# A graph attention layer over 196 groups of edges: gathering every group, shorter look-ahead, and maxima in three parts

## The chip, the cores and the metric

The kernel runs on one core of a Trainium2 chip. The metric is the device time of one execution in microseconds (us). The core's engines are named as in the profile: PE (TensorE, matrix products; PEld are its weight loads), DVE (VectorE), ACT (ScalarE), POOL (GpSimd, which here issues the indirect loads) and SP (SyncE, which issues most other loads and stores). Each works through its own list of instructions in order, and waits where one needs something that another engine or a transfer has not yet delivered.

## The reference

3125 nodes with 128 features, 100000 edges sorted by destination, 5 relations, 8 heads of 16. For each relation, a softmax over the edges that arrive at a node weighs the sources' values; the sums go through a projection, a residual and two normalisations. Cut to what matters:

```python
x_src = node_embeddings[src]
x_dst = node_embeddings[dst]
for r in range(R):
    mask = edge_types == r
    q = jnp.einsum('eh,khd->ekd', x_dst, W_Q[r])
    k = jnp.einsum('eh,khd->ekd', x_src, W_K[r])
    v = jnp.einsum('eh,khd->ekd', x_src, W_V[r])
    logits = (q * k).sum(-1) / scale + attn_bias[r][None, :]
    masked_logits = jnp.where(mask[:, None], logits, NEG)
    max_v = jax.ops.segment_max(masked_logits, dst, num_segments=n)
    exp_l = jnp.where(mask[:, None], jnp.exp(masked_logits - max_v[dst]), 0.0)
    sum_exp = jax.ops.segment_sum(exp_l, dst, num_segments=n)
    attn = exp_l / (sum_exp[dst] + 1e-12)
    out = out + jax.ops.segment_sum(attn[:, :, None] * v, dst, num_segments=n)
```

## The kernel before

**Tables first.** For every node and relation, k and v (256 numbers, 1 KB) and q (in three bf16 parts) are computed once and stored in DRAM (`kv_d`, `q_d`). The preparation, up to about 111 us, makes the table of k and v for all 25 blocks of 128 nodes (`table`, L398), the first three blocks of q, and the lists of indices and of destinations.

**Groups and steps.** The edges are cut into 196 groups of 512, each held as 128 partitions by T = 4 columns. The main loop (L1124) counts steps k. In step k the group g = k gets its logits, and an older group v gets its softmax weights and sums:

- `gather(g)` (L694): four indirect loads on POOL, one a column, each bringing 128 rows of k and v from `kv_d` into a buffer `kvs_[g % KVB]`. There are KVB = 23 buffers. Before the loop the first KVA = 9 groups are gathered (L1121); then in step k the loop gathers up to the group of step k + AHEAD, AHEAD = 3 (L1150), in the last steps one step ahead.
- `fetch_keys`, `fetch_q` (SP): the group's keys and a window of 128 rows of `q_d`, three steps ahead. `spot` (DVE, L795) makes one-hot matrices `hot`, `spread_q` (PE, L804, 12 matmuls) spreads q over the edges, `logits` (DVE, L817 and L818) multiplies by k and sums over each head, `store_logits` (SP, L823) writes them to `lg_d`.
- When all edges of a block of 128 nodes have logits (step `full_step[b]`, called F below, every 8 steps), `maxima_load(b)` in step F + 1 fetches for each node its run of up to 64 edges' logits (`ell`, one indirect load on POOL, L830). On POOL it stands behind the gathers of its step. `maxima(b, c0, c1)` computes the relations' maxima: ACT copies `ell` into `by_head` (PSUM, L845), DVE makes a mask `mine` (L853), for each relation a row `shut` (L863), adds (`wl`, L868) and reduces (`mx`, L874); the last part also rounds into three bf16 pieces (L879 to L889). It is called with relations 0 to 2 in step F + 3 and 3 to 4 in step F + 4 (`ready[b]` is F + 8). `store_m` writes the result in step F + 5.
- 16 to 19 steps after its logits, a group is weighed: `spread_m` (PE, L921) spreads the maxima, `less_max` (DVE, L930), `exps` (ACT, L934), `weigh` (DVE, L939, the last reader of the group's buffer), `sums` (PE, L973) with a carry between groups, `norm` (DVE, L994 to L997), `by_node` (ACT, L1007). The first weighing is in step 16.

Within a step DVE's order is: weigh, less_max, norm, logits, spot, pieces of q's later blocks, then maxima, then normalisations of finished blocks.

**The XG groups.** Groups 3, 6, 9, 12 and 15 (`XG`, L62) are not gathered from the table. Their source nodes' x is gathered during the preparation (L653 to L658) into buffers that exist from the start, together with those of groups 0, 1, 2 and 4. Five steps before such a group is due, PE turns x (`turn_x`, L764), DVE makes five copies masked by relation (`by_relation`, L771, `xm`), PE multiplies them with the weights (`products`, L782, `pk`) and ACT copies k and v into the buffer (`put_kv`, L791), spread over four steps, with the edges' types loaded by SP (L757).

Of the kernel before, what the change touches and what calls it, by code (L numbers as in the profile page):

```python
# [17 lines left out]
P = 128  # L18
N = 3125
NT = 25  # L20
NP = NT * P
R = 5
HEADS = 8
HD = 16
H = 128
# [5 lines left out]
KVW = 2 * H  # L31
# [8 lines left out]
GE = 512  # L40
T = GE // P
NGR = -(-E // GE)
# [6 lines left out]
RH = 3  # L49
# [1 line left out]
LW = HEADS + 1  # L51
PW = H + HEADS
FAR = 4000
AHEAD = 3
LAG = 8
LAG_H = 7
HALVED = 0
# [1 line left out]
NSR = E // SR  # L59
SB = P * E // N // SR  # L60
SPAD = 5
XG = range(3, 16, 3)  # L62
QB = 3
KVB = 23
HELD = 21
KVA = 9

# [66 lines left out]
def windowed_path(  # L134
# [4 lines left out]
    nc = tc.nc  # L139
# [11 lines left out]
    def keep(name, shape, dt=F32):  # L151
        return const.tile(shape, dt, name=name)
# [15 lines left out]
    lift = keep("lift", [1, H])  # L168
    wq = keep("wq", [P, R, H])
    wkv = keep("wkv", [P, R, 2, H])  # L170
    xi = keep("xi", [P, len(XG), T], I32)

    kvs_ = {}

    def buffers(those):
        for i in those:
# [1 line left out]
                [P, T, KVW], F32, name=f"kv{i}"  # L178
            )


    at_once = [*(g for g in range(5) if g not in XG), *XG]
    buffers(at_once)
    ahead = ctx.enter_context(tc.tile_pool(name="ahead", bufs=3))

# [7 lines left out]
    xn = load.tile([P, NT, H], F32, name="xn")  # L193
    nc.vector.memset(xn[:, NT - 1, :], 0.0)
    nc.sync.dma_start(xn[:, :4, :], x[: 4 * P].rearrange("(i p) h -> p i h", p=P))
    nc.sync.dma_start(
        xi,
        src[: (NGR - 1) * GE].rearrange("(g p t) -> p g t", p=P, t=T)[
            :, XG.start : XG.stop : XG.step, :
        ],  # L200
    )
    fr = load.tile([1, NGR + NSR], I32, name="fr")
    with nc.allow_non_contiguous_dma(reason="one element of each group"):
        nc.sync.dma_start(
# [30 lines left out]
    ident = keep("ident", [P, P])  # L235
# [125 lines left out]
    live = {}  # L361
# [287 lines left out]
        15: [sorted_rows],  # L649
        17: [sorted_ends],  # L650
    }

    for i, g in enumerate(XG):  # L653
        for t in range(T):
            nc.gpsimd.indirect_dma_start(
                out=kvs_[g][:, t, H:], out_offset=None, in_=x[:, :],
                in_offset=bass.IndirectOffsetOnAxis(ap=xi[:, i, t : t + 1], axis=0),
            )  # L658
    rows, counted = {}, 0
    xT = {b: turn(b) for b in range(2)}  # L660
    for b in range(NT):
# [27 lines left out]
    ps = ctx.enter_context(tc.tile_pool(name="ps", bufs=2, space=PSUM))  # L689
# [2 lines left out]
    flow = ctx.enter_context(tc.tile_pool(name="flow", bufs=2))  # L692
    late_flow = ctx.enter_context(tc.tile_pool(name="late_flow", bufs=2))
    def gather(g):  # L694
        if g in XG:
            return
        kv = kvs_[g % KVB]
        for t in range(T):
            nc.gpsimd.indirect_dma_start(  # L699
                out=kv[:, t, :], out_offset=None, in_=kv_d[:, :],  # L700
                in_offset=bass.IndirectOffsetOnAxis(ap=idx[:, t, g : g + 1], axis=0),
            )
# [43 lines left out]
    def store_q(b):  # L746
# [8 lines left out]
    def fetch_types(g):  # L755
        tr = ahead.tile([P, GE], I32, name="tr", bufs=1)
        nc.sync.dma_start(tr, edge_type[g * GE : (g + 1) * GE].partition_broadcast(P))  # L757
        live["tr", g] = tr

    def turn_x(g):  # L760
        xe = kvs_[g % KVB][:, :, H:]
        tx = ps.tile([P, T, P], F32, name="tx", tag="me")
        for t in range(T):
            nc.tensor.transpose(tx[:, t, :], xe[:, t, :], ident)  # L764
        live["tx", g] = tx

    def by_relation(g):
        tr, tx = live.pop(("tr", g)), live.pop(("tx", g))
        xm = late_flow.tile([P, R, T, P], F32, name="xm", tag="wl", bufs=1)
        for r in range(R):  # L770
            nc.vector.scalar_tensor_tensor(  # L771
                xm[:, r], tr.rearrange("h (p t) -> h t p", t=T), float(r), tx,
                op0=ALU.is_equal, op1=ALU.mult,
            )
        live["xm", g] = xm

    def products(g, t0):
        xm = live["xm", g]
        pk = ps.tile([P, 2, KVW], F32, name="pk", tag="me")
        for t in range(2):  # L780
            for r in range(R):
                nc.tensor.matmul(  # L782
                    pk[:, t, :], xm[:, r, t0 + t, :], wkv[:, r].rearrange("h s c -> h (s c)"),
                    start=(r == 0), stop=(r == R - 1),
                )
        if t0:
            live.pop(("xm", g))
        live["pk", g, t0] = pk

    def put_kv(g, t0):  # L790
        nc.scalar.copy(kvs_[g % KVB][:, t0 : t0 + 2, :], live.pop(("pk", g, t0)))  # L791

    def spot(g):
        hot = hold.tile([WR, T, P], BF16, name="hot")
# [281 lines left out]
    step_of, n = {}, 0  # L1076
# [24 lines left out]
    root_at = {b: d + 2 for b, d in done_at.items()}  # L1101
# [4 lines left out]
    norm_at = {b: r + (r < final - 1) for b, r in root_at.items()}  # L1106


    x_at = {g: step_of[g] - 5 for g in XG}
    assert min(x_at.values()) >= -2 and max(x_at.values()) + 2 < at_k[0] - 1  # L1110
# [10 lines left out]
    for gathered in range(KVA):  # L1121
        gather(gathered)
    assert all(q_from[b] >= 2 for b in range(QB, NT))
    for k in range(-4, root_at[NT] + 2):  # L1124
        v, g = v_at.get(k), group_at.get(k)
        q_step = {k - f: b for b, f in enumerate(q_from) if b >= QB and -2 <= k - f <= 5}

        if k >= 0 and k + 3 in group_at:
            fetch_keys(group_at[k + 3])
            fetch_q(group_at[k + 3])  # L1130
        if -2 in q_step:
            fetch_x("xq", q_step[-2])
        for b in range(NT):
            if done_at[b] - 1 == k:
                fetch_x("xr", b)
            if norm_at[b + 1] + 1 == k:
                store_z(b)
        for b in range(NM):
            if ready[b] - 3 == k:
                store_m(b)  # L1140
        if 5 in q_step:
            store_q(q_step[5])
        for u in range(NGR):
            if max(at_k[u] - 3, ready[block_of(u, MEND)] - 2) == k:
                fetch_m(u)
        for u in XG:
            if x_at[u] - 2 == k:
                fetch_types(u)

        while gathered < NGR - 1 and step_of[gathered + 1] <= k + (AHEAD if k < final - 16 else 1):  # L1150
            gathered += 1
            gather(gathered)
        for b in range(NM):
            if full_step[b] + 1 == k:
                maxima_load(b)

        for u in XG:
            if x_at[u] + 2 == k:
                put_kv(u, 0)
                put_kv(u, 2)  # L1160
        for b in range(NT):
            if done_at[b] + 1 == k:
                residual(b)
        if v_at.get(k - 4) is not None:
            by_node(v_at[k - 4])
        if v_at.get(k - 2) is not None:
            carry(v_at[k - 2])
        if 1 in q_step:
            turned(q_step[1])
        if 3 in q_step or 4 in q_step:  # L1170
            second_part()
        if 2 in q_step or 3 in q_step:
            first_part()

        if v_at.get(k + 1) is not None:
            spread_m(v_at[k + 1], 8 if k + 1 in group_at else 12)
        if v_at.get(k - 1) is not None or v_at.get(k - 3) is not None:
            sums(v_at.get(k - 1), v_at.get(k - 3))
        if k + 1 in group_at:
            spread_q(group_at[k + 1])  # L1180

        if v is not None:
            weigh(v)
        if v_at.get(k + 1) is not None:
            less_max(v_at[k + 1])
            exps(v_at[k + 1])
        if v is not None:
            weights(v)
        if k + 1 in group_at:
            types(group_at[k + 1])  # L1190
        if v_at.get(k - 2) is not None:
            norm(v_at[k - 2])
        if g is not None:
            logits(g)
            store_logits(g)
        if k + 2 in group_at:
            spot(group_at[k + 2])
        if v_at.get(k + 1) is not None:
            places(v_at[k + 1], 2 if k >= final - 1 else 0)
        if 3 in q_step or 4 in q_step:  # L1200
            third_part()
        if 2 in q_step or 3 in q_step:
            remainder()
        for b in range(NM):
            whole = MB[b][2] is None
            if ready[b] - 5 == k and whole:
                maxima(b, 0, RH)
            if ready[b] - 4 == k:
                maxima(b, RH if whole else 0, R)
        for b in range(NT):  # L1210
            if done_at[b] == k:
                project(b)
        for b in range(NT + 1):
            if root_at[b] == k:
                roots(b)
            if norm_at[b] == k:
                norms(b)
        for u in XG:
# [517 lines left out]
```

## Time and profile before

| | us |
|---|---|
| median of 3 runs | 1664.48 |
| lowest, highest | 1659.51, 1679.92 |
| the profiled execution, its own time | 1665.2 |
| its span in the profile | 1663.5 |

| engine | busy us | share of the span | instructions |
|---|---|---|---|
| PE | 1043.0 | 63% | 7746 |
| PEld | 790.5 | 48% | 7746 |
| DVE | 945.4 | 57% | 2536 |
| ACT | 638.7 | 38% | 2258 |
| POOL | 796.5 | 48% | 901 |

No engine is busy all the time. In the profile's other parts, a line such as `L699 POOL DMA_INDIRECT kv<-kv_d,idx x764 | 724.5, 948 | 587.9` names a line of the kernel, the engine, the operation, what it writes and reads, how often; then the busy time in us, the mean of one in ns, and how long the engine was idle just before. For an indirect load POOL's time is that of issuing it, not of the transfer. The mean granted clock of PE was 0.724 of full speed.

The groups that the change touches:

| group | count | busy us | mean ns |
|---|---|---|---|
| L699 kv gathers, POOL | 764 | 724.5 | 948 |
| L655 x gathers for XG, POOL | 20 | | 944 (median) |
| L830 ell, POOL | 25 | 23.6 | 944 |
| L782 pk, PE | 200 | 62.9 | 448 |
| L868 wl, DVE | 49 | 73.1 | 1491 |

### The profile page before, as it was taken

How to read it: one execution, taken by the hardware profiler on the slowest of the kernel's cores; microseconds unless marked ns; L12 is line 12 of the kernel's file. 1: busy time of each engine (PE TensorE's matmuls, PEld its weight loads, DVE VectorE, ACT ScalarE, POOL GpSimd, SP SyncE). 2: the span in 40 equal slices, each digit the busy share in tenths (PEclk: the TensorE clock that was granted, in tenths of full speed). 3: DMA queues.
4: the chain of work that ended last, by engine and by line, in shares of the span. 5: the costliest groups of instructions: out<-in, count | busy, mean ns of one | idle time of the engine just before them, and what ended most of it. 6: DMA issues, size and time to landing. Idle time of an engine off the chain costs nothing.

```text
span 1663.5 us, 26129 instructions
## 1 busy us (share of the span) xinstructions
PE 1043.0 (63%) x7746; PEld 790.5 (48%) x7746; DVE 945.4 (57%) x2536; ACT 638.7 (38%) x2258; POOL 796.5 (48%) x901
## 2 busy tenths in 40 slices
PE   6774836356566666665666666666566655665676
PEld 2443624245454444554554554555445544454564
DVE  3452626455564665556466555657555564564686
ACT  1450103144344444434445443444344343334344
POOL 6345061645465545545645554555455455445400
PEclk8885967677676767667676766777666776666878
DMA  6683343445455544544545454555445444444400
GB/s 161 232 309 105 72 134 80 108 124 137 101 135 126 132 110 121 137 109 118 144 118 129 126 137 107 137 131 131 108 120 139 109 122 120 107 118 108 102 16 15
DMA packets 181946, 203.66 MB, mean 122 GB/s; under 512 B 83943, under 2 KB 146819, under 8 KB 181676
## 3 DMA queue, kind: packets, MB, share of 16 engines
q0 software_dynamic: 40576, 112.08, 23.4%
q1 hardware_dynamic: 136790, 85.12, 21.9%
q10 hardware_dynamic: 4430, 4.71, 1.1%
q8 instruction: 64, 1.05, 0.3%
q14 instruction: 86, 0.70, 0.1%
HBM read 166.51 MB, written 35.28 MB: 121 GB/s over the span
## 4 chain that ended last, share of the span: by engine, by line
PE 29%; DVE 28%; issue 19%; another core or an unknown queue 10%; ACT 5%; DMA 2%; SPq 1%; DVEq 0%; ACTq 0%; POOL 0%
PE pp L973 9%; PE qe L804 4%; PE me L921 4%; DVE wl L868 4%; DVE mx L874 4%; DVE prod L817 4%; PE pk L782 3%; DVE wv L939 3%; DVE lg L818 2%; PE pp L975 2%; PE pr L404 2%; ACT at L959 2%; DVE hot L795 2%; PE prq L725 1%
## 5 line engine op out<-in xcount | busy, mean ns | idle before, releaser
L699 POOL DMA_INDIRECT kv<-kv_d,idx x764 | 724.5, 948 | 587.9 <-DVE den L994 346.6
L973 PE MATMUL pp<-wv,at 128*125 128x136 f32 x1568 | 392.7, 385 | 43.3 <-issue 34.1
L973 PEld LDWEIGHTS pp<-wv,at 128*125 128x125 f32 x1568 | 295.7, 256 | 122.4 <-issue 116.0
L804 PE MATMUL qe<-qw,hot 125*128 125x128 bf16 x2352 | 229.9, 256 | 87.7 <-issue 77.6
L921 PE MATMUL me<-mw,hot 125*128 125x64 bf16 (+1 forms) x2352 | 145.3, 217 | 217.6 <-issue 115.2
L804 PEld LDWEIGHTS <-hot 125*128 125x128 bf16 x2352 | 203.3, 125 | 99.6 <-issue 86.3
L921 PEld LDWEIGHTS <-hot 125*128 125x128 bf16 x2352 | 126.6, 113 | 253.5 <-issue 197.0
L934 ACT ACTIVATE me<-me 128x32 f32<-128x32 f32 x196 | 35.7, 182 | 542.0 <-DVE me L930 409.5
L959 ACT ACTIVATE at<-row_at,nkey 128x125 f32<-128x125 f32 x744 | 237.6, 398 | 0.0
L930 DVE TENSOR_TENSOR me<-lg,me 128x32 f32<-128x32 f32 x196 | 37.7, 193 | 348.6 <-remote 195.6
L939 DVE TENSOR_TENSOR wv<-kv,me 128x512 f32<-128x512 f32 x196 | 133.0, 679 | 104.0 <-remote 63.2
L817 DVE TENSOR_TENSOR prod<-kv,qe 128x512 f32<-128x512 f32 x196 | 132.9, 678 | 43.2 <-PE qe L804 25.7
L818 DVE TENSOR_REDUCE lg<-prod 128x32 f32<-128x512 f32 x196 | 134.5, 686 | 6.8
L975 PE MATMUL pp<-pt,carried 125*5 125x136 f32 x390 | 101.4, 350 | 57.8 <-ACT pt L988 27.4
L962 ACT ACTIVATE at<-at 128x500 f32<-128x500 f32 (+1 forms) x196 | 117.3, 599 | 6.2
L725 PE MATMUL prq<-wq,xTq 128*128 128x384 f32 (+1 forms) x88 | 52.7, 693 | 92.9 <-DVE hot L795 61.1
L1007 ACT COPY oT<-pp 128x25 f32 x196 | 33.7, 172 | 180.6 <-PE me L921 72.8
L830 POOL DMA_INDIRECT ell<-lg_d,start_i x25 | 23.6, 944 | 154.3 <-DMA lg_d<-lg 62.0
L782 PE MATMUL pk<-wkv,xm 128*128 128x256 f32 x200 | 62.9, 448 | 50.3 <-issue 46.3
L868 DVE TENSOR_TENSOR wl<-by_head,shut 128x1536 f32<-128x1536 f32 (+2 forms) x49 | 73.1, 1491 | 33.7 <-PE pk L782 25.6
L982 PEld LDWEIGHTS pp<-rsum,o 125*128 125x128 f32 x392 | 83.6, 257 | 14.0 <-issue 13.3
L982 PE MATMUL pp<-rsum,o 125*128 125x25 f32 x392 | 74.2, 270 | 12.8 <-issue 8.2
(191 smaller groups left out, 1199.5 us busy)
## 6 DMA issues: line engine op xcount, KB each, us to landing
kt<-key_d SPq DMA_DIRECT2D x196, 128.0 KB
qw<-q_d SPq DMA_DIRECT2D x196, 96.0 KB
kv_d<-kvs SPq DMA_DIRECT2D x24, 640.0 KB
kv<-kv_d,idx POOLq DMA_INDIRECT x764
q_d<-q SPq DMA_DIRECT2D x22, 480.0 KB
lg_d<-lg SPq DMA_DIRECT2D x196, 18.0 KB
mw<-m_d SPq DMA_DIRECT2D x196, 6.0 KB
xr<-in_x SPq DMA_DIRECT2D x24, 64.0 KB
```

What stands on the lines that cost most here:

```text
L699: nc.gpsimd.indirect_dma_start(out=kv[:, t, :], out_offset=None, in_=kv_d[:, :], in_offset=bass.IndirectOffsetOnAxis(ap=idx[:, t, g : g + ...
L804: nc.tensor.matmul(qe[:, t, :], hot[:, t, :], qw[:WR, s, :], start=(s == 0), stop=(s == 2))
L817: nc.vector.tensor_tensor(prod, kv[:, :, :H], live.pop(("qe", g)), op=ALU.mult)
L818: nc.vector.tensor_reduce(lg[:, :, :HEADS], prod.rearrange("p t (k d) -> p t k d", d=HD), AX.X, ALU.add)
L868: nc.vector.tensor_tensor(wl, by_head[:, None].to_broadcast([P, n, nh, D]), shut[:, :n, None, :].to_broadcast([P, n, nh, D]), op=ALU.add,)
L921: nc.tensor.matmul(me[:, t], hot[:, t, :], mw[:WR, None, :, s, :].to_broadcast([WR, times, 2, HEADS // 2]), start=(s == 0), stop=(s == 2),)
L939: nc.vector.tensor_tensor(wv[:, :, :H].rearrange("p t (k d) -> p t k d", d=HD), kv[:, :, H:].rearrange("p t (k d) -> p t k d", d=HD), live ...
L959: nc.scalar.activation(at[:, t, :], row_at[:, :WR], AF.Abs, bias=nkey[:, t, g : g + 1], scale=1.0)
L962: nc.scalar.activation(at[:, on_dve:], at[:, on_dve:], AF.Relu, bias=1.0, scale=-1.0)
L973: nc.tensor.matmul(pp, at[:, t, :], wv[:, t, :], start=(t == 0), stop=(t == T - 1))
L975: nc.tensor.matmul(pp[:R], carried[:WR, g, :], live.pop(("pt", g - 1)), start=False, stop=False,)
L982: nc.tensor.matmul(op, live.pop(("o5", done)), rsum[:WR], start=True, stop=True)
```

## The change

1. `XG` and all that belongs to it is taken out: the list of indices `xi` and its load, the 20 gathers of x, `fetch_types`, `turn_x`, `by_relation`, `products`, `put_kv` and their places in the loop. Groups 3, 6, 9, 12 and 15 are gathered from `kv_d` like the others. The buffers that exist from the start are now those of groups 0 to 8, and all nine of these groups are gathered before the loop.
2. `AHEAD` goes from 3 to 2, `KVB` from 23 to 22.
3. The maxima of a whole block are computed in three parts: relations 0 and 1 in step F + 2, 2 and 3 in step F + 3, 4 and the rounding in step F + 4.

```diff
-AHEAD = 3
+AHEAD = 2
...
-XG = range(3, 16, 3)
 QB = 3
-KVB = 23
+KVB = 22
...
-    at_once = [*(g for g in range(5) if g not in XG), *XG]
+    at_once = range(KVA)
...
-    nc.sync.dma_start(
-        xi,
-        src[: (NGR - 1) * GE].rearrange("(g p t) -> p g t", p=P, t=T)[
-            :, XG.start : XG.stop : XG.step, :
-        ],
-    )
...
-    for i, g in enumerate(XG):
-        for t in range(T):
-            nc.gpsimd.indirect_dma_start(
-                out=kvs_[g][:, t, H:], out_offset=None, in_=x[:, :],
-                in_offset=bass.IndirectOffsetOnAxis(ap=xi[:, i, t : t + 1], axis=0),
-            )
...
     def gather(g):
-        if g in XG:
-            return
         kv = kvs_[g % KVB]
...
-    x_at = {g: step_of[g] - 5 for g in XG}
...
-    for k in range(-4, root_at[NT] + 2):
+    for k in range(-2, root_at[NT] + 2):
...
-        for u in XG:
-            if x_at[u] + 2 == k:
-                put_kv(u, 0)
-                put_kv(u, 2)
...
+            if ready[b] - 6 == k and whole:
+                maxima(b, 0, 2)
             if ready[b] - 5 == k and whole:
-                maxima(b, 0, RH)
+                maxima(b, 2, 4)
             if ready[b] - 4 == k:
-                maxima(b, RH if whole else 0, R)
+                maxima(b, 4 if whole else 0, R)
...
-        for u in XG:
-            if x_at[u] == k:
-                turn_x(u)
-                by_relation(u)
-            if x_at[u] + 1 == k:
-                products(u, 0)
-                products(u, 2)
```

More of the change, by code (lines that the diff above doesn't have):

```diff
@@ L170, in windowed_path @@
     wkv = keep("wkv", [P, R, 2, H])
-    xi = keep("xi", [P, len(XG), T], I32)
     kvs_ = {}
@@ L751, in store_q @@
         )
[L755 to L791, printed above, removed]
     def spot(g):
@@ L1106, in windowed_path @@
     norm_at = {b: r + (r < final - 1) for b, r in root_at.items()}
-    x_at = {g: step_of[g] - 5 for g in XG}
-    assert min(x_at.values()) >= -2 and max(x_at.values()) + 2 < at_k[0] - 1
     q_from = []
@@ L1145, in windowed_path @@
                 fetch_m(u)
-        for u in XG:
-            if x_at[u] - 2 == k:
-                fetch_types(u)
         while gathered < NGR - 1 and step_of[gathered + 1] <= k + (AHEAD if k < final - 16 else 1):
@@ L1217, in windowed_path @@
                 norms(b)
-        for u in XG:
-            if x_at[u] == k:
-                turn_x(u)
-                by_relation(u)
-            if x_at[u] + 1 == k:
-                products(u, 0)
-                products(u, 2)
         if 0 in q_step:
```

## The prediction

> **What bounds the kernel now.** I read the busy table of chosen stretches first, because the change touches two different stages: the start (before the first group is weighed) and the steady loop. Columns: stretch, its length, then busy time of each engine with its count of instructions, granted clock, DMA share, GB/s.
>
> ```profile
> core 0: us, PE busy (x) PEld busy (x) DVE busy (x) ACT busy (x) POOL busy (x), PEclk, DMA share, GB/s
> 111.50:156.70 45.20, 19.07 (x65) 13.02 (x65) 14.19 (x42) 2.88 (x9) 34.49 (x36) 0.58 0.55 166
> 156.70:205.20 48.50, 40.95 (x238) 30.82 (x238) 30.26 (x45) 6.51 (x20) 0.02 (x1) 0.89 0.27 61
> 205.20:246.10 40.90, 16.68 (x84) 11.86 (x83) 9.24 (x16) 2.25 (x6) 31.15 (x33) 0.70 0.49 139
> 246.10:284.10 38.00, 22.19 (x180) 16.54 (x180) 23.57 (x50) 12.26 (x43) 0.05 (x2) 0.68 0.26 56
> ```
>
> POOL alternates: 36 gathers back to back (1.25 us each), 48 us of nothing, 33 more, nothing. While it gathers, everyone else nearly stands still (PE 65 matmuls in 45 us, against 238 in the next 48). The timeline of PE inside the first burst shows how: matmuls trickle out one per 1.4 to 2.8 us, "issue" before each, waiting for nothing the trace names.
>
> ```profile
> 135.45 0.38 PE L782 MATMUL pk<-wkv,xm 128*128 128x256 f32 x1 [1.60 <-issue]
> 137.55 0.59 PE L782 MATMUL pk<-wkv,xm 128*128 128x256 f32 x1 [1.73 <-issue]
> 139.66 0.59 PE L782 MATMUL pk<-wkv,xm 128*128 128x256 f32 x1 [1.52 <-issue]
> ```
>
> Third, the chain of waits between the first gather (111.46) and the first weighing (273.46), and the list of who waited for whom:
>
> ```profile
> by line: issue 34.0%; PE pk L782 28.4%; DVE xm L771 10.5%; PE qe L804 3.4%; DVE prod L817 2.0%; DVE wl L868 1.8%; DVE mx L874 1.8%; DMA kv<-kv_d,idx 1.5%; DVE lg L818 1.3%; DMA mw<-m_d 1.2%; PE hp L540 1.1%; DVE q3s L622 0.9%; DVE hot L795
> ```
>
> ```profile
> POOL kv L699 <- DVE den L994: 346.6, 85, 11.0
> ...
> POOL ell L830 <- ACT kv L791: 48.5, 1, 48.5
> ```
>
> Of 164 us at the start, 28.4% (47 us) are the matmuls that build rows of k and v for the five XG groups, 10.5% (17 us) the masked copies that feed them: work that exists only because these groups are not gathered. POOL's 48.5 us is the logits row load of block 0 (ell), which waits until step 8 is through.
>
> Steady loop, 401 to 1462 us: loads of ell at 401.1 and 1461.9 bound 18 blocks, 58.9 us each, about 7.4 us a step. POOL's 346.6 us on DVE are its pacing: the buffer for a gather comes free with a weighing. Block 9 is typical: ell issues at 755.24 (late, after waiting for the logits of step 81), then 12 gathers follow without a pause to 771.3, and DVE is idle 764.5 to 773.9 waiting for a trickling PE. Isolated runs of four gathers (5.0 us) with 2 us behind them mostly show no such stall; runs of 8 show 2.3 to 7.5 us, of 13 9 to 14 us. So what bounds a block is DVE and PE work in open stretches plus these stalls.
>
> **The change part by part.** Time before of the profiled execution: 1665.2 us (span 1663.5), 0.7 above the median of three, 1664.48; the sum is made on 1665.2.
>
> *XG groups.* Removed: 5 groups x (5 masked copies of 0.99 us, 40 matmul passes of 0.22 us undisturbed, 4 transposes, 2 copies of 0.585 us on ACT), their type loads, and 20 gathers of x between 11.8 and 37.2 us. Those 20 stand in front of the row gathers of the preparation (first at 37.73, 0.5 us behind them); the chain there is the table's matmuls (L404), so I count this at 0, at most 0.5 us. Added: 20 gathers from the table, 25 us of POOL, nine groups instead of seven ahead of the loop. Before, ell of block 0 stood behind 36 table gathers, now behind 48 (groups 0 to 11). The 12 more fit into POOL's 48.5 idle us; what they cost is a longer first burst, 111.5 to 171.5.
>
> Floor: if gathers alone set the pace, step 16 (first weighing) needs 17 groups x 5.0 us + ell 1.25 + about 2.4 landing (the DMA piece at 207.67 in the chain): 111.5 + 88.7 = 200, gain 73 us. Ceiling: XG's work was all hidden behind the trickle and 12 + 4 more gathers (4 more in the second burst) lengthen it: 20 us lost. In between, by the rows: step 0 to 2 before the trickle starts (134), then about 13 us a step (12 matmuls of qe took 10.5 us in the trickle at 414.6 to 425.1, plus waits), three steps to 175 (the trickle ended 4 us after the first burst), three free steps at 2.6 us (step 8 to 9 before) to 183, store and wait 4 us: ell at 187 instead of 205.2. Second burst 37 x 1.25 to 233 instead of 246; steps 12 to 14 pass inside it, the rest 4 us + two steps of 5: first weighing near 247 instead of 273.5. I take **26 us gained**, ends 20 lost and 73 gained; nearer the middle because both bursts have their like in the trace.
>
> The Trainium skill's page "Runtime: NRT & Kernel Launch", section on instruction fetch mechanics, says engines fetch instructions in 16 KiB blocks over a DMA queue of their own and that this is mostly hidden. The trickle speaks against that being so beside gathers, if fetching is its cause, which no row here proves. By the rule there would be no trickle and the start would go to the floor, 1665.2 - 73 - 17 = 1575; by the rows it is the sum below.
>
> *Gathers two steps ahead, 22 buffers.* In step k the gather is for k+2 instead of k+3; its buffer was last read in the weighing of group k-20 in both versions, which is step k-1. So POOL's releases do not move: each gather issues when its neighbour did and serves a group one step earlier. In block 9 the slot at 756.5 to 760.2 now fills group 85, used at 782.1; in the tightest place of the steady loop, between the last gather of such a slot and the product that would use it, 10 us are left, against 2.4 for a landing. Counted at 0; if a faster loop used that up, one landing a block, 22 x 2.4 = 53 us. On POOL ell now has one group fewer in front of it, which matters only at the start (above). The last 17 steps gather one step ahead in both.
>
> *Maxima in three parts.* Durations by form:
>
> ```profile
> L868 DVE TENSOR_TENSOR wl<-by_head,shut 128x1536 f32<-128x1536 f32 x1 | 1.8, 1757 | 0.3 <-ACT by_head L845 0.3
> L874 DVE TENSOR_REDUCE mx<-wl 128x24 f32<-128x1536 f32 x1 | 1.8, 1753 | 0.0
> L868 DVE TENSOR_TENSOR wl<-by_head,shut 128x1024 f32<-128x1024 f32 x1 | 1.2, 1224 | 0.0
> L874 DVE TENSOR_REDUCE mx<-wl 128x16 f32<-128x1024 f32 x1 | 1.2, 1220 | 0.0
> ```
>
> 512 elements cost 0.53 us and a start 0.16, so a part of one relation is 0.69 + 0.69. With F the step that completes a block: F+3 had 0.33 + 0.40 + 3.51 = 4.23 us, F+4 2.74 and 1.3 of rounding. Now F+2 gets 3.06, F+3 2.74, F+4 1.55 and the 1.3. In block 9, DVE is full from the product of step 84 (774.6) to that of 86 (789.1), so these two steps shorten by 1.49 and 1.19 us, if PE (4 us) and POOL (5.0 us a group) are not late next: the steps go to 6.0 and 5.8. The 3.06 us go where DVE then stands idle from 764.5. That cover is there in 16 of the blocks 1 to 22 (step F+3 comes 7.9 us or more after F+2); in six it follows in 4 to 6.4 us and the net is 0.38 lost. Sum: 16 x 2.68 - 6 x 0.38 = 41 us at best. What stands against it: steps of 6 us leave POOL under 1 us between groups, and runs join to 8. I take 40%, **17 us**, ends 41 gained and the second rival's loss. The added wait is ACT's copy by_head, one step sooner, with ACT's carry, exps and DVE's weighing queued behind it: ell's packets end 3 to 4 us after its issue; in blocks 1, 2 and 7 that is 0.5 to 2 us behind the new place, some 5 us in all, inside the 40%.
>
> Sum: 1665.2 - 26 - 17 = **1622**.
>
> **Rivals.** (1) *The bursts eat it*: the 48 gathers hold the start in the trickle, which gives back the 26 us, and the joined runs take the 17. For it: the four stretches above, where gathering and progress exclude each other; against it: POOL's 48.5 idle us. Time 1650, between 1632 and 1690. (2) *Slower*: at steps F+4 and F+5 POOL no longer pauses, each block's run of 4 + 4 becomes one of 8 to 12, with a stall of 5 to 8 us against the 2.7 saved: 22 x 2.3 to 5.3 = 50 to 117 us, less 15 from the start: 1700 to 1767. It decides when the pause falls under about 1 us. For it: runs of 8 with stalls exist; against: the delayed weighing in F+3 parts the run of 13 into 9 + 4, which should shorten the longest stall. (3) *Nothing at the start*: ell of block 0 does not move from 205, as something else of steps 0 to 8 (SP's loads) sets it; then 1665 - 17 = 1648, counted with (1).
>
> **How the numbers follow.** Two per cent, about what a measurement of this kernel tells from no change, is 33 us: 1631 and 1698 about the median. Forecast (own range 1585 to 1635) 0.53, of which 0.01 lies above 1631; rivals 1 and 3 together 0.28; rival 2 0.19. Range: 1585 (start half way to its floor) to 1695, which leaves out nearly all of rival 2. Faster 0.52, same 0.29, slower 0.19.
>
> **What would show it.** Right: ell of block 0 near 187, first weighing near 247, no rows of tx, xm, pk; POOL's first run 48, second 37. Steady blocks near 58 us, steps F+4 and F+5 near 6 us, by_head in step F+2 without idle before it. Wrong: first weighing after 265; more than one run of 12 gathers in a block; POOL's wait on DVE well under 346 us with a block longer than 59 us; products waiting for a gather's landing.

## The result, and the profile after

| | before | after |
|---|---|---|
| median of four runs each, us | 1668.98 | 1592.82 |
| lowest, highest | 1659.51, 1679.92 | 1588.83, 1600.05 |
| the profiled execution | 1665.2 | 1596.71 |
| its span | 1663.5 | 1594.9 |

The ratio is 0.9546, interval 0.947 to 0.9623: faster by 4.5 per cent. Ratios and their 95 per cent intervals, here and below, are formed from undisturbed executions alone, so they are not exactly the quotients of the medians. The forecast was 1622, with a range from 1585 to 1695. The sign was right, and the two parts that were to gain did gain, though not altogether in the way forecast; the gain, from the 1665.2 us that the sum started from, was 72 us against 43.

First the view that the prediction began with: busy time of each engine in the two bursts of gathers and the two stretches behind them, now in the kernel after.

```profile
core 0: us, PE busy (x) PEld busy (x) DVE busy (x) ACT busy (x) POOL busy (x), PEclk, DMA share, GB/s
89.10:148.80 59.70, 7.65 (x50) 6.88 (x50) 9.37 (x37) 3.38 (x15) 45.38 (x48) 0.52 0.49 142
148.80:174.30 25.50, 13.03 (x110) 10.43 (x111) 16.56 (x32) 2.53 (x10) 0.21 (x1) 0.59 0.49 91
174.30:221.50 47.20, 7.27 (x58) 5.30 (x55) 14.43 (x30) 1.67 (x5) 34.98 (x37) 0.53 0.53 144
221.50:243.00 21.50, 10.55 (x129) 9.25 (x130) 13.25 (x31) 10.63 (x38) 0.12 (x1) 0.74 0.32 69
```

The bursts have 48 and 37 indirect loads (the second begins with the load of ell), as counted beforehand, and in the first one PE starts 50 matmuls in 60 us: gathers and progress still exclude each other. By parts of the burst it is more of a standstill than a trickle:

```profile
105.00:120.00 15.00, 0.00 (x0) 0.00 (x0) 0.00 (x0) 0.00 (x0) 11.34 (x13) 0.50 0.37 105
130.00:150.00 20.00, 0.00 (x0) 0.00 (x0) 0.00 (x0) 0.00 (x0) 14.44 (x16) 0.50 0.39 113
```

The first product is made at 122.2 us, the second at 154.3, behind the burst. What shrank is the stretch between the bursts (25.5 us instead of 48.5), since nothing is left to be computed for the XG groups. And everything begins earlier: the first gather at 89.06 us instead of 111.46. The load of ell of block 0 is at 174.3 (205.2 before), the first weighing at 232.2 (273.5 before).

Then the list of who waited for whom, and the pieces of the maxima by form:

```profile
POOL kv L681 <- DVE den L936: 252.9, 58, 11.1
...
POOL ell L772 <- DMA lg_d<-lg: 52.4, 5, 22.6
...
ACT by_head L787 <- DMA ell<-lg_d,start_i: 10.1, 4, 6.3
...
PE qe L746 <- DMA kv<-kv_d,idx: 1.8, 1, 1.8
```

```profile
L810 DVE TENSOR_TENSOR wl<-by_head,shut 128x1024 f32<-128x1024 f32 x48 | 58.8, 1225 | 15.8 <-issue 10.3 <-ACT by_head L787 2.0 <-DVE shut L805 1.3
L816 DVE TENSOR_REDUCE mx<-wl 128x16 f32<-128x1024 f32 x48 | 58.6, 1220 | 1.6
L810 DVE TENSOR_TENSOR wl<-by_head,shut 128x512 f32<-128x512 f32 x24 | 16.6, 692 | 0.8
L816 DVE TENSOR_REDUCE mx<-wl 128x8 f32<-128x512 f32 x24 | 16.5, 686 | 0.8
```

The small part takes 0.692 + 0.686 us; 0.69 + 0.69 was worked out. The copy by_head, put one step sooner, waits for its load in 4 of 25 blocks, 10.1 us in all. POOL's wait on DVE is down from 346.6 to 252.9 us. Waiting for a gather's landing is next to nothing, with one step less to land in.

Where the time went, by marks in the two traces: 22.4 us before the first gather; 18.9 us from there to the first weighing (273.5 - 111.5 = 162.0, now 232.2 - 89.1 = 143.1); 27.3 us from the first weighing to the end (1390.0 to 1362.7). Together 68.6, as much as the spans differ by (68.5). The loads of ell of blocks 3 to 21 are 58.9 us apart before and 57.2 after.

### The profile page after: what moved, and what is told of

It is laid out like the page before. It is cut to its first block, busy times and chain, and to the rows that moved or that the text cites. A ratio compares the mean times of both kernels' runs of the same rounds, so it can differ in the third digit from the quotient of the medians.

```text
span 1594.9 us, 25686 instructions
## 1 busy us (share of the span) xinstructions
PE 978.5 (61%) x7526; PEld 752.9 (47%) x7526; DVE 931.1 (58%) x2559; ACT 636.1 (40%) x2248; POOL 797.2 (50%) x901
## 5 line engine op out<-in xcount | busy, mean ns | idle before, releaser
L681 POOL DMA_INDIRECT kv<-kv_d,idx x784 | 742.5, 947 | 534.3 <-DVE den L936 252.9
L915 PE MATMUL pp<-wv,at 128*125 128x136 f32 x1568 | 399.6, 386 | 68.3 <-issue 62.1
L746 PE MATMUL qe<-qw,hot 125*128 125x128 bf16 x2352 | 235.3, 261 | 139.9 <-issue 69.1
L863 PE MATMUL me<-mw,hot 125*128 125x64 bf16 (+1 forms) x2352 | 150.4, 217 | 237.5 <-issue 112.2
L746 PEld LDWEIGHTS <-hot 125*128 125x128 bf16 x2352 | 207.9, 127 | 158.4 <-issue 89.0
L863 PEld LDWEIGHTS <-hot 125*128 125x128 bf16 x2352 | 130.9, 114 | 264.6 <-issue 232.9
L901 ACT ACTIVATE at<-row_at,nkey 128x125 f32<-128x125 f32 x744 | 237.5, 398 | 0.0
L759 DVE TENSOR_TENSOR prod<-kv,qe 128x512 f32<-128x512 f32 x196 | 132.8, 678 | 83.2 <-remote 62.1
L707 PE MATMUL prq<-wq,xTq 128*128 128x384 f32 (+1 forms) x88 | 48.5, 639 | 81.0 <-DVE rem L717 59.9
L949 ACT COPY oT<-pp 128x25 f32 x196 | 33.7, 172 | 135.9 <-remote 89.1
L810 DVE TENSOR_TENSOR wl<-by_head,shut 128x1024 f32<-128x1024 f32 (+2 forms) x73 | 76.9, 1053 | 17.2 <-issue 10.3
L816 DVE TENSOR_REDUCE mx<-wl 128x16 f32<-128x1024 f32 (+2 forms) x73 | 76.5, 1048 | 2.5
```

The lines of the kernel that those rows point to most:

```text
L681: nc.gpsimd.indirect_dma_start(out=kv[:, t, :], out_offset=None, in_=kv_d[:, :], in_offset=bass.IndirectOffsetOnAxis(ap=idx[:, t, g : g + ...
L746: nc.tensor.matmul(qe[:, t, :], hot[:, t, :], qw[:WR, s, :], start=(s == 0), stop=(s == 2))
L759: nc.vector.tensor_tensor(prod, kv[:, :, :H], live.pop(("qe", g)), op=ALU.mult)
L810: nc.vector.tensor_tensor(wl, by_head[:, None].to_broadcast([P, n, nh, D]), shut[:, :n, None, :].to_broadcast([P, n, nh, D]), op=ALU.add,)
L863: nc.tensor.matmul(me[:, t], hot[:, t, :], mw[:WR, None, :, s, :].to_broadcast([WR, times, 2, HEADS // 2]), start=(s == 0), stop=(s == 2),)
L901: nc.scalar.activation(at[:, t, :], row_at[:, :WR], AF.Abs, bias=nkey[:, t, g : g + 1], scale=1.0)
```

## The experiments

There are twelve runs, in four sittings, each beside the kernel before on the same chip. One sitting differs so much from the others that it has to be told first. In three of them, as in the first measurement, the kernel before took 1660 to 1684 us. In the second it took 1217.58 us (1211.38 to 1223.0), and all four kernels of that sitting ran at that pace. Five minutes later the same chip gave 1683.81. The cause isn't known. These four kernels speak for that condition only, and are kept apart, under "the quick sitting".

**1. The XG groups alone taken out** (look-ahead 3, 23 buffers, two parts of maxima stay).

```diff
-XG = range(3, 16, 3)
...
     def gather(g):
-        if g in XG:
-            return
```

> The kernel before with the XG groups taken out and nothing else (three steps ahead, 23 buffers, maxima in two parts). Theory (XG is the whole of the early gain: 22 us in the preparation, 19 us between the first gather and the first weighing): first gather near 89, first weighing near 232, time 1665 - 41 = 1624, within 8. Rival (the shorter look-ahead, not XG, moved the start): first weighing stays above 250 and the time above 1640.

Measured: 1610.88 us beside 1659.74, ratio 0.9693 (0.9631 to 0.9755). The first gather is at 88.8 us, ell of block 0 at 178.5, the first weighing at 233.6. So nearly the whole gain at the start, the part before the first gather included, comes from this edit: 39.9 us against 41.3 in the kernel after. The time is 13 us under what was expected, 48.9 under that of before by the medians. The rest lies behind the first weighing, where this kernel has the loop of before, maxima included, and yet blocks of 57.5 us. In its second run (experiment 7) they are 59.5 us: from one trace to another a block can differ by 2 us with nothing changed.

**2. The maxima alone in three parts, one step sooner.**

```diff
+            if ready[b] - 6 == k and whole:
+                maxima(b, 0, 2)
             if ready[b] - 5 == k and whole:
-                maxima(b, 0, RH)
+                maxima(b, 2, 4)
             if ready[b] - 4 == k:
-                maxima(b, RH if whole else 0, R)
+                maxima(b, 4 if whole else 0, R)
```

> The kernel before with the maxima in three parts one step sooner, nothing else. Theory (DVE work moved under the idle stretch of step F + 3): blocks of 58.9 us become about 57.5 to 58, total 15 to 30 us less, 1635 to 1650. Rival (the steady gain comes from elsewhere, a part more only costs its start, 0.38 us a block): 1665 to 1673.

Measured: 1619.07 us, ratio 0.9737 (0.9675 to 0.9799), which is 44 us, 33 to 54 by the interval (41 by the medians): more than expected. Blocks are 57.0 us apart. From the first weighing to the end its trace takes 1348.6 us, 41.4 less than before.

**3. Look-ahead 2 and 22 buffers alone.**

```diff
-AHEAD = 3
+AHEAD = 2
...
-KVB = 23
+KVB = 22
```

> The kernel before with gathers two steps ahead into 22 buffers, nothing else. Theory (releases on POOL do not move): same, 1655 to 1675, steady blocks 58.9 us within 0.5. Rival (one group fewer ahead of ell on POOL shortens the runs of gathers): blocks 58 us or less and 1645 or less; the other way, products that wait for a landing: over 1680.

Measured: 1673.16 us, ratio 1.0068 (1.0027 to 1.0108): 11 us lost, 4 to 18 by the interval, and inside the time expected. What loses them isn't shown. Its ten times fall apart, three from 1655.76 to 1660.67 us and seven from 1672.48 to 1681.39, and the trace is of the 1660.67: that no product waits for a landing in it, and that its blocks are 58.6 us, tells only of an execution that lost nothing.

**4. The 20 x gathers spread over the table's blocks**, one with each of the blocks 2 to 21, in place of one run at the start.

```diff
-    for i, g in enumerate(XG):
-        for t in range(T):
-            nc.gpsimd.indirect_dma_start(
...
+        if 2 <= b < 2 + len(XG) * T:
+            i, t = divmod(b - 2, T)
+            nc.gpsimd.indirect_dma_start(
```

> The kernel before with its 20 gathers of x issued one with each block of the table (blocks 2 to 21) instead of all at 11.8 to 37.2 us; same gathers, same bytes. Theory (it is the run of gathers back to back that slows the preparation): first gather of k and v near 92, time about 1665 - 20 = 1645. Rival (the gathers' transfers, or the load of their indices, cost the time wherever they stand): first gather stays near 111, time near 1665.

Measured: 1660.36 us, ratio 0.9997 (0.9957 to 1.0037), first gather at 105.5 us instead of 111.5. Most of the expected gain stayed away. The busy times of 50 to 75 us tell why, first of this kernel, then of the kernel after:

```profile
50.00:75.00 25.00, 15.25 (x49) 8.31 (x50) 3.91 (x8) 9.10 (x25) 16.53 (x18) 0.80 0.58 200
```

```profile
50.00:75.00 25.00, 24.53 (x86) 14.19 (x87) 12.97 (x28) 17.71 (x49) 11.00 (x12) 1.00 0.94 355
```

Up to about 50 us the table runs like that of the kernel after. But the spread gathers fall between those that belong to the table (dr), 18 instead of 12 in this stretch, and from 30.8 to 65.5 us POOL issues 26 gathers without a pause. PE makes 49 matmuls instead of 86, and none from 55 to 60 us. Spreading moved the run; it didn't part it.

**5. The x gathers put back into the kernel after**, with the load of their indices and nothing that uses them: they write into the buffers of groups 3 to 7, which the row gathers fill later. It ran twice; the first time in the quick sitting (below).

```diff
+    nc.sync.dma_start(
+        xi, src[: (NGR - 1) * GE].rearrange("(g p t) -> p g t", p=P, t=T)[:, 3:16:3, :]
+    )
...
+    for g in range(3, 8):
+        for t in range(T):
+            nc.gpsimd.indirect_dma_start(
+                out=kvs_[g][:, t, H:], out_offset=None, in_=x[:, :],
+                in_offset=bass.IndirectOffsetOnAxis(ap=xi[:, g - 3, t : t + 1], axis=0),
+            )
```

> The changed kernel with the 20 gathers of x and the load of their indices put back into the preparation, once more: its first run met the condition in which the kernel before takes 1218 us and nothing stands still beside gathers, and the first row gather then came at 96.7 us, 5 to 9 us behind its neighbours without the x gathers. Theory (the 22.4 us in the preparation are these gathers, holding up every engine): if before is near 1670, the first row gather goes from 89-90 back to 109-112 us, and the ratio is 1.3 per cent above the changed kernel's 0.955 and 0.967: 0.966 to 0.982. Rival (the gain came from the other things taken out): first row gather at 89 to 96 us and the changed kernel's ratio. If before is near 1218 again: 1247 us and 96.7 us again.

Measured: 1615.45 us beside 1660.13, ratio 0.9733 (0.9634 to 0.9831), as the theory had it. The timeline of POOL at the first row gather, first of this kernel, then of the kernel after (start, duration, what, idle before and what ended it):

```profile
110.48 0.95 POOL L691 DMA_INDIRECT kv<-kv_d,idx  x1 [13.50 <-DMA kv_d<-kvs]
```

```profile
89.06 0.95 POOL L681 DMA_INDIRECT kv<-kv_d,idx  x1 [13.59 <-DMA kv_d<-kvs]
```

It comes 21.4 us later, and the first weighing 21.3 later (253.5). In both it waits for the table's last store, so it is the table that is late. Its busy times from 11.8 to 47.4 us and on to 89, in the kernel before, in this one, and in the kernel after:

```profile
11.80:47.40 35.60, 20.80 (x52) 8.53 (x50) 10.58 (x29) 5.34 (x13) 27.14 (x28) 0.71 0.50 153
47.40:89.00 41.60, 36.84 (x120) 20.51 (x121) 21.86 (x43) 21.74 (x59) 12.54 (x14) 0.88 0.71 270
```

```profile
11.80:47.40 35.60, 19.96 (x52) 8.46 (x50) 11.35 (x32) 5.34 (x13) 26.54 (x28) 0.71 0.52 155
47.40:89.00 41.60, 38.62 (x123) 21.45 (x124) 21.80 (x41) 22.61 (x62) 13.05 (x13) 0.88 0.73 277
```

```profile
11.80:47.40 35.60, 31.64 (x106) 16.83 (x105) 23.28 (x55) 14.53 (x37) 13.22 (x12) 0.95 0.69 240
47.40:89.00 41.60, 39.64 (x134) 22.00 (x131) 20.13 (x43) 28.35 (x82) 13.05 (x14) 1.00 0.90 338
```

POOL's column tells them apart: 28 instructions, 20 of x and 8 of dr, nearly without a pause, against 12. PE makes 52 matmuls with them and 106 without, DVE 29 or 32 instructions against 55. Neither x nor its product is needed before the loop. The load of the indices, put back with the gathers, isn't the cause: the kernel of experiment 4 has it in the same place, and makes 105 matmuls in the first of these stretches:

```profile
11.80:47.40 35.60, 31.35 (x105) 16.80 (x104) 23.28 (x55) 14.39 (x37) 13.21 (x12) 0.95 0.72 246
```

So it is the run of gathers that holds up the table. Its length matters: the kernel after issues 13 gathers of dr nearly without a pause from 30.8 to 49.3 us, and PE makes 59 matmuls beside them in 18.5 us. In the kernel before the standstill comes late in the run of 28, with 5 matmuls from 35 to 50 us.

**6. The two old parts of the maxima, each one step sooner**, in the kernel before: steps F+2 and F+3, nothing in F+4. This parts the place from the division. It too ran twice, the first time in the quick sitting.

```diff
-            if ready[b] - 5 == k and whole:
+            if ready[b] - 6 == k and whole:
                 maxima(b, 0, RH)
-            if ready[b] - 4 == k:
+            if ready[b] - 4 - whole == k:
                 maxima(b, RH if whole else 0, R)
```

> The kernel before with its two parts of the maxima one step sooner (steps F+2 and F+3), once more under the other condition, if before is near 1670. Theory (the place pays: work out of the full steps into the stretch where the vector engine waits for trickling matrix products): as much as three parts gave alone, ratio 0.974 or less (0.960 to 0.980), blocks near 57 us. Rival (the division into smaller pieces pays): ratio 0.985 to 1.0, blocks near 58.5 us. If before is near 1218 again: ratio 1.037 again, 1265 us.

Measured: 1690.25 us, ratio 1.0237 (1.0147 to 1.0327): slower than before. Both theories had it at 1.0 or less, so both fell. Mean time up to the product of each step from the product before, in blocks 3 to 20, in us (the maxima of a step come behind its product, so those of F+4 fall under F+5):

| | F+1 | F+2 | F+3 | F+4 | F+5 | F+6 | F+7 | F+8 | block |
|---|---|---|---|---|---|---|---|---|---|
| before | 6.44 | 6.56 | 11.33 | 7.41 | 7.03 | 5.62 | 7.46 | 7.07 | 58.9 |
| after | 3.99 | 7.27 | 9.88 | 6.95 | 6.78 | 8.94 | 5.40 | 8.02 | 57.2 |
| three parts alone | 5.03 | 7.25 | 9.61 | 6.62 | 7.20 | 7.97 | 5.29 | 8.00 | 57.0 |
| two parts, sooner | 6.06 | 7.34 | 10.67 | 7.01 | 3.08 | 14.30 | 4.06 | 7.02 | 59.5 |

The differences under F+1 to F+3 prove little: the two traces of the kernel without XG groups, which has the maxima of before, stand at 6.04 and 10.50 us under F+2 and at 10.93 and 8.88 under F+3. The two columns that the edit aims at are clear. The step that lost its maxima is done in 3.08 us, as hoped; the next takes 14.30. The timelines of POOL, DVE and PE in block 9 of this kernel show what happens:

```profile
778.95 0.95 POOL L699 DMA_INDIRECT kv<-kv_d,idx  x1 [2.31 <-DVE den L994]
780.20 0.94 POOL L699 DMA_INDIRECT kv<-kv_d,idx  x1 [0.30 <-issue]
...
783.96 0.94 POOL L699 DMA_INDIRECT kv<-kv_d,idx  x1 [0.30 <-DVE hot L795]
...
792.72 0.95 POOL L699 DMA_INDIRECT kv<-kv_d,idx  x1 [0.30 <-issue]
```

```profile
784.70 0.69 DVE L939 TENSOR_TENSOR wv<-kv,me 128x512 f32<-128x512 f32 x1 [0.33 <-PE qe L804]
796.16 0.20 DVE L930 TENSOR_TENSOR me<-lg,me 128x32 f32<-128x32 f32 x1 [10.77 <-remote]
```

```profile
787.48 0.35 PE L973 MATMUL pp<-wv,at 128*125 128x136 f32 x1 [0.46 <-issue]
788.87 0.28 PE L975 MATMUL pp<-pt,carried 125*5 125x136 f32 x1 [1.04 <-issue]
790.98 0.39 PE L975 MATMUL pp<-pt,carried 125*5 125x136 f32 x1 [1.82 <-issue]
```

Weighings at 778.0, 780.9 and 784.7 release three buffers so fast that POOL, 5.0 us a group, never pauses: one run of twelve from 778.95. PE trickles under it, "issue" before each matmul, and DVE stands for 10.77 us ("remote" names no releaser inside the core). Between the loads of ell of blocks 3 and 21 this kernel has 16 runs of twelve, the kernel before 2, three parts alone none (of twelve or more: 19, 8 and 4). This is the prediction's second rival, which the change as made escapes: its step F+4 keeps the last relation and the rounding, and 6.8 to 7.2 us pass until the product of F+5.

POOL's wait on DVE puts the two side by side, first three parts, then two parts sooner:

```profile
POOL kv L699 <- DVE den L994: 230.8, 63, 10.9
```

```profile
POOL kv L699 <- DVE den L994: 340.7, 77, 11.6
```

Whether three parts at the old place would do as well wasn't tried.

**7. The kernel after, and the one without XG groups, once more**, on the chip of the quick sitting, to see them there.

> The changed kernel itself once more. The four runs before this one ran on another chip, where the kernel before takes 1218 us instead of 1660, its engines do not stand still while gathers run, and each version with the maxima one step sooner was slower than before (1.020 to 1.037). Theory: on such a chip the copy of the logits rows, one step sooner, waits for its load 22 times (69 us in all in the version with look-ahead 3), and that costs more than the start saves. If this run meets that condition (before near 1218), the changed kernel is at 1235 to 1248 us, ratio 1.015 to 1.025, with blocks of 44 us and the copy waiting 50 us or more. Rival: what was slower there came from what was put back or from the look-ahead of 3; then the changed kernel is at or under 1218 us. If before is near 1660, the ratio is 0.955 again and the copy waits less than 15 us in all.

> The kernel before without the five groups computed from x, everything else as before (maxima in two parts, steps F+3 and F+4). Theory: the start gains on every chip, and only the maxima one step sooner lose where nothing else stands still. If before is near 1218: first weighing near 185 us instead of about 207, blocks near 42 us instead of 44, time 1195 us (1185 to 1205), ratio 0.98, so faster than the changed kernel by 4 per cent. Rival: the loss there comes from the gathers themselves (20 more of them, a longer first run); then this kernel too is at or over 1218 us. If before is near 1660: ratio 0.97 as measured once, and 1.5 per cent slower than the changed kernel.

By then the kernel before took 1683.81 us again, so the question about the quick condition got no answer. The kernel after: 1634.67 us, ratio 0.9668 (0.9596 to 0.974). Without XG only: 1654.07, ratio 0.9828 (0.9785 to 0.987), first gather at 89.0 us, first weighing at 237.5. The two stand to each other as before (0.9546 / 0.9693 = 0.985; 0.9668 / 0.9828 = 0.984), but each has gained less. A gain of this size moves by more than a per cent from sitting to sitting and chip to chip, for the kernel without XG groups beyond the interval of either (0.9631 to 0.9755, 0.9785 to 0.987).

**8. The quick sitting.** Four kernels, beside 1217.58 us of before. The one with x kept is the edit of 5, the one with the maxima sooner that of 6. The other two are the kernel after with

```diff
+    for g in (3, 4):
```

in place of the five groups of 5 (8 x gathers kept, and the load of all 20 lists of indices), and the kernel after with

```diff
-AHEAD = 2
+AHEAD = 3
...
-KVB = 22
+KVB = 23
```

> The changed kernel, with 20 gathers of x and the load of their indices put back at the start of the preparation (they write into buffers that the row gathers fill later, so nothing reads what they bring). Theory: the 22.4 us by which the first row gather came sooner are the cost of these gathers alone, which ran back to back with eight others in the preparation and held up every engine. Then the first row gather goes from 89 back to 110-112 us, the blocks stay near 57 us, and the time is 1593 + 22 = 1615 us (1608 to 1622). Rival: the gain in the preparation came from what else was taken out (the buffers that exist from the start, the two steps ahead of the loop); then the first row gather stays at 89 to 92 us and the time at 1593 +- 6 us.

> The changed kernel with the load of the 20 lists of indices and 8 of the 20 gathers of x put back. Theory (each gather in the run costs its share): 8/20 of 22.4 us, so the first row gather at 98 us (95 to 101) and the time near 1602 us. Rival (the load of the indices, scattered 4 bytes at a time, holds up the other loads): as with all 20, first row gather at 108 to 112 us and 1615 us. Second rival (a run only stalls the others past a certain length): first row gather at 89 to 91 us and 1593 us.

> The changed kernel with the look-ahead of three steps and the 23 buffers of before: nothing gathered in place of x, maxima in three parts. Theory (the parts add up): alone they gave 0.9693 and 0.9737 of the time of before, together 0.9438, which is 1566 us beside 1660 of before (1560 to 1580), so faster than the changed kernel's 0.9546 by about one per cent. Rival (the parts share one gain in the steady loop, 58.9 to 57 us a block with either): 0.955 to 0.965 of before, 1585 to 1602 us.

> The kernel before with the two parts of the maxima as they were (relations 0 to 2, then 3 and 4), but each one step sooner, in steps F+2 and F+3; step F+4 has none. Theory (the place is what pays: work moved out of the full steps F+3 and F+4 into the stretch where the vector engine waits): 4.0 us less in F+4, the 4.2 us of F+2 hidden, so at least what three parts gave: 1595 to 1622 us beside 1660 of before. Rival (the division pays: smaller pieces let the weighing, and with it the release of the buffers, come sooner): the long pieces keep holding it up, less than half of that gain, 1640 to 1665 us.

| | us | ratio | interval | first gather | first weighing | block |
|---|---|---|---|---|---|---|
| x kept | 1247.31 | 1.0257 | 1.0206 to 1.0309 | 96.7 | 186.8 | 44.2 |
| 8 x gathers kept | 1242.46 | 1.0204 | 1.0132 to 1.0276 | 88.1 | 177.2 | 44.3 |
| look-ahead 3 | 1245.27 | 1.0223 | 1.0174 to 1.0273 | 91.6 | 184.5 | 44.2 |
| two parts, sooner | 1265.15 | 1.0371 | 1.0312 to 1.0429 | 97.0 | 207.2 | 44.3 |

None of the expectations was made for this and none can be judged by it. What differs is best seen where the same kernel (two parts sooner) issues the same run of gathers, in stretches of equal length, first in the quick sitting, then in the later one:

```profile
99.90:141.20 41.30, 33.04 (x188) 25.94 (x189) 23.36 (x55) 3.80 (x14) 31.24 (x34) 0.79 0.67 193
```

```profile
112.80:154.10 41.30, 18.66 (x63) 12.47 (x63) 11.63 (x36) 0.85 (x4) 31.26 (x33) 0.58 0.56 162
```

POOL is as busy, its gathers start 1.25 us apart in both, yet PE makes 188 matmuls against 63. Beside these gathers the standstill is gone. In the preparation a part of it stays: from 35 to 45 us the kernel with x kept makes 10 matmuls, the one with look-ahead 3, which has no x gathers, 34. So x kept costs less than in experiment 5, but not nothing (first gather 96.7 us against 88.1 with eight x gathers and 91.6 with none). In the loop the empty step F+4 starts no stall (F+5 3.03, F+6 4.30 us), and POOL, at 33 loads of 1.25 us in a block of 44.2, is close to being the bound itself.

And there all four are slower than the kernel before. Each has the maxima one step sooner, the fourth as its only change. The copy by_head then does wait, as in the list of waits of the version with look-ahead 3:

```profile
ACT by_head L787 <- DMA ell<-lg_d,start_i: 69.3, 21, 17.2
```

Twenty-one waits, against 4 and 10.1 us in the kernel after above. That this wait is what costs the per cents is not shown: the slowest of the four, two parts sooner, waits there for 37.1 us in all and the others for 63.5 to 69.3, no trace of the kernel before was taken there, and neither the changed kernel itself nor the one without XG groups ran under that condition.

## Why the prediction was right in sign, and short in size

| step of the sum | predicted | measured |
|---|---|---|
| x gathers in the preparation | 0, at most 0.5 | -22.4; 21.4 when put back |
| the rest of the start | -26 | -18.9 |
| look-ahead and buffers | 0 | +11, alone |
| maxima in three parts | -17 | -44, alone |
| sum | -43 | -74 |

The first two rows are read from the traces before and after, the last two are whole kernels measured alone. Measured together it was 76 us by the medians, 72 from the 1665.2 of the forecast and 68.5 by the spans. With the 48.9 us of the XG groups measured alone in place of the 41.3 from the traces, the parts come to 82. So they nearly add up, within what sittings and traces differ by.

*The step that failed: "the chain there is the table's matmuls (L404), so I count this at 0, at most 0.5 us".* The chain was read rightly, and so was the fact that the x gathers end 0.5 us ahead of the row gathers of the preparation. What was not asked is whether the table's matmuls themselves go slower beside a run of gathers. The prediction's first fence said so for 111 to 157 us (65 matmuls in 45 us); the same columns for 11.8 to 47.4 us, shown under experiment 5, were there to be read. A rule found in one stretch was not applied to another.

*The start, -26.* The mechanism held: bursts of 48 and 37, and ell at 85.3 us from the first gather instead of 93.7. That gave 8.4 us where 18.2 were counted, because less is done beside the gathers than assumed. Three steps were to be through before the trickle and three more by 4 us behind the first burst; one product was made by then, at 122.2 us, and the rest of the steps up to ell was done behind the burst, in 25.5 us. No row shows three steps so early: in the kernel before, too, the first product is made only at 146.7 us, inside the burst. From ell to the first weighing it took 57.8 us against the 60 counted. The x gathers and the rest of the start being two terms, the sum of both, 41.3, lies inside the bounds given for the rest alone (20 lost, 73 gained).

*The Trainium skill's rule* ("Runtime: NRT & Kernel Launch", section on instruction fetch mechanics: fetching is mostly hidden) stood for a start at the floor, 1575. Beside gathers the trickle stayed in every sitting but the quick one. The share of the larger instruction queue is 0.3% of the DMA engines' time in the quick and in the later run of the same kernel alike. The trace's list of DMA packets says more: in the kernel before no packet of an instruction queue starts between 10.5 and 62.1 us, the stretch that holds the standstill of the preparation and its end, and in the kernel after two do between 89.1 and 148.8 us, for 50 matmuls, at 97.8 and 125.5. No standstill there ends with one. So the recorded fetches don't pace the trickle, and the forecast's doubt of the rule, which it made hang on fetching being the cause, finds no support in these records.

*The maxima, -17.* This term was mis-sized too: 41 times 40 per cent, where 44 (33 to 54) was measured alone. That the 41 before the deduction comes so near is luck, for the places named were not where it came from: F+4 and F+5 went to 6.95 and 6.78 us, not to 6.0 and 5.8, F+6 rose by 3.3, and F+1, F+3 and F+7 fell by 2.45, 1.45 and 2.06. So it isn't the saving on DVE in F+4 and F+5 that was counted. What the trace gives instead: the stretches over 1.5 us, from 400 to 1500 us, in which neither DVE nor ACT works add up to 337.6 us before, 277.1 with three parts alone and 284.7 in the kernel after, and POOL's wait on DVE falls with them. That this comes from weighings spread more evenly is a reading, not shown; the kernel without XG groups, with the old maxima, has 314.7 us.

*The 60 per cent taken off* were for runs that join. Experiment 6 shows that this loss is real, 2.4 per cent, and where it begins: when one step has no maxima left and its weighings come 3 to 4 us apart. The change stays clear of that.

*Look-ahead, 0.* It costs 11 us alone, by an unknown way: the one trace, in which no product waits for a landing, is of an execution that did not lose them. The kernel after with a look-ahead of 3 ran in the quick sitting alone, so whether it beats the kernel after in the other condition is open.

*The rivals.* The first (the bursts eat it) fell because 18.9 us were gained from the first gather to the first weighing, and because the maxima alone gained. The third (ell does not move) fell too, though by less than ell at 174.3 suggests: 22.4 of its 30.8 us are the earlier first gather. The second did not come true, but its mechanism exists.

## What to carry to other kernels

Where one stretch of a profile shows that an engine's work slows all others, read the same columns in every other stretch where that engine runs without a pause; work "off the critical path" there may be what makes the path long. When moving work out of a full step, look at what the emptied step sets free, and how fast: three pieces gained 2.6 per cent, two pieces that emptied a step lost 2.4. And a gain that rests on a stall belongs to the condition that shows the stall: where it was mostly absent, kernels with the maxima one step sooner were 2 to 4 per cent slower.

## What the runs showed of the hardware

- A long run of indirect gathers, 1.25 us from start to start, holds up the other engines. In the preparation 28 of them leave PE 52 matmuls instead of 106 in 35.6 us, while a run of 13 (30.8 to 49.3 us in the kernel after) holds up nothing. In the loop of the kernel before, runs of eight already show it: beside each of 22 such runs DVE and ACT both rest for 2.4 to 7.6 us on end.
- No load that the trace shows ends these standstills. In the kernel after, SP's next load and DVE's first product, at 122.13 and 122.19 us, follow a signal of PE that by the trace's semaphore records comes at 122.11, and the second product, at 154.32, follows one at 154.30, though the records of the 24 matmuls behind these two signals end at 104.55 (their ends are modelled). SP's sequencer, too, takes 1.40 us from one instruction to the next there (105.25, 106.65 and 108.05 us), and behind the burst no more than 0.4 (156.64, 156.95 and 157.03 us). Whether the instructions run late or only their signals, and what holds them, stayed open, as did whether it also happens in an execution that no profiler records.
- This is not always so. On one chip, five minutes apart, the kernel before took 1217.58 and 1683.81 us, and with the same pace of gathers a kernel that ran in both conditions made 188 and 63 matmuls in 41.3 us beside them. What sets the condition stayed open.
